# Cross-attention with folded weights: first weight loads by rows, context's rest turned by VectorE, Wv turned into a tile of its own

## The chip, the core and the metric

The kernel runs on one core of a Trainium2 chip. The core has five engines that run at the same time, each through its own list of instructions in order: TensorE (PE; its weight loads are shown apart as PEld), VectorE (DVE), ScalarE (ACT), GpSimd (POOL) and SyncE (SP), which here only issues DMAs. The metric is the device time of one execution in microseconds (us). The kernel before takes 280.88 us, the median of three runs (280.25 to 281.27).

## What is computed

Sixteen batches; x is 256 x 256 per batch, the context c is 77 x 192 per batch, with 8 heads of width 256. All in float32.

```python
Q = (x @ Wq)    # 256 -> 8 heads of 256
K = (c @ Wk)    # 192 -> 8 heads of 256
V = (c @ Wv)
score = einsum("bhqd,bhkd->bhqk", Q, K) / sqrt(256)
score = where(mask, score, -inf)
attn = softmax(score)
out = (attn @ V) @ Wo + x
y = (out - mean(out)) * rsqrt(var(out) + 1e-5) * gamma + beta
```

## The kernel before

Weights are folded first. For each head, `Wk` of the head times `Wq` of the head, transposed, gives a 192 x 256 matrix, kept as `gA` (its first 128 rows) and `gB` (its last 64); `Wv` times `Wo` of the head gives `uA` and `uB` in the same way. `Q`, `K` and `V` are never formed. The context is held transposed: `cA` has its first 128 features on the partitions, `cB` the last 64, twice (a copy on the other half of the partitions). `cRA` and `cRB` hold the columns of the last 13 keys of each batch.

The program has two parts. The first, some 57 us of the span, is the preparation, and the second is a loop over the 16 batches (scores, softmax, product with the values, sum with x, layer norm) with TensorE busy throughout. The loop's first instruction on TensorE is `scores` (tile ps, L313). The change lies in the preparation alone.

The schedule is by hand: each engine does its instructions in the order in which the program names them, and waits on semaphores for what it needs. On TensorE the preparation runs in this order:

1. Idle transposes of the identity (`keep_busy`, L605), 14 at first, until weights land.
2. `turn_k`, `turn_q`, `turn_k_last` (L619): the first two heads of each half of the eight are loaded in natural layout and transposed 128 x 128 by TensorE (tiles pt_k, pt_q, pt_kl); an ACT or DVE copy takes each result to `kT` or `qT`. The index e is a pair of neighbouring heads (heads 0 and 1, or 4 and 5), u the head in the pair, t the upper or lower 128 rows of Wq.
3. `g_of(e)` (tile pg, L723) and `rest_of_g(u)` (tile ph, L737): the folded products of these heads.
4. `turn_c` (tile pc, L657): the context's rows in `c_sb`, 112 to a row of tiles, are transposed by TensorE; ACT copies to `cA`, DVE to the upper half of `cB`, POOL from there to its lower half. The first call does 3 of the 11 rows, which is enough for the first four batches.
5. `a_of_places` (tile pa, L199 and L213): products of `gA` and `gB` with the context of the first four batches.
6. `of_pair` and `rest_of_pairs` (L680, L694) for the other heads of Wk and Wq (tiles pgb and phb). These weights come in blocks of 32 x 32, turned by DVE (`turn_blk`, L646) out of `wk_blk` and `wq_blk` into `kT_blk` and `qT_blk`.
7. Once more `a_of_places`, then `turn_c` for the other 8 rows.
8. The same `of_pair` and `rest_of_pairs` with Wv and Wo (tiles pu and pw). `turn_v` (L672) turns Wv's blocks in place in `wvT`; `wv_part` reads columns with a step of four elements.
9. `prepare_last` (tile pr, L274 and L284): `uA` and `uB` with `cRA` and `cRB`, into `vr`.

POOL meanwhile copies `cRA` and `cRB` (L784, L785), clears `vr` (L786), turns the mask into the additive `bias` (L790), copies halves of `uB` (L809), forms differences in `uA` and `uB` (L812, L813), and adds the mask's NaN rule to `bias` (L818), which the loop's first `shift` on DVE (L328) reads.

All loads are issued by SP on one queue, in program order: Wk and Wq for e = 0, then for e = 1, the last 64 rows of Wk (`wk_last`), three rows of context, the blocks of Wk and Wq, the other eight rows of context, Wv's blocks, Wo, mask, and the first group of x in blocks (`load_xT`). Eight semaphores are used in turn for them, so an issue waits until the eighth load before it has landed. PSUM has eight banks (`ps_mm`), reused in turn.

Of the kernel before, what the change touches and what calls it, by code (L numbers as in the profile page):

```python
# [8 lines left out]
F32 = mybir.dt.float32  # L9
I32 = mybir.dt.int32  # L10
AF = mybir.ActivationFunctionType
ALU = mybir.AluOpType
# [3 lines left out]
P = 128  # L16
H = 8
D = 256
EPS = 1e-05
GB = 4  # L20
KM = 64
MASKED = 3.0e38
# [31 lines left out]
def kernel(  # L54
# [13 lines left out]
    nc = tc.nc  # L68
    B, S, DI = x.shape
    S2, DL = c.shape[1], c.shape[2]  # L70
    LB = DL - P
    CR = 112
    NCR = B * S2 // CR
    NG = B // GB
    QT = S // P
    NT = B * QT
# [5 lines left out]
    NL = DL // BK  # L82
    PW = (NF + 1) * BK
    assert KM == 2 * BK and NM == NF and 2 * KR <= BK
    assert NCR * CR == B * S2 and NG * GB == B and DI == 2 * P and D == 2 * P and 2 * LB == P


    engines = mybir.EngineType
# [30 lines left out]
    cB = const.tile([P, B, S2], F32, tag="cB", name="cB")  # L119
    cRA = const.tile([P, B, KR], F32, tag="cRA", name="cRA")  # L120
    cRB = const.tile([P, B, KR], F32, tag="cRB", name="cRB")
    vr = const.tile([P, B, DI], F32, tag="vr", name="vr")
    p_ring = [const.tile([P, NM, PW], F32, tag=f"p{i}", name=f"p_{i}") for i in range(2)]
    for p in p_ring:
        nc.gpsimd.memset(p[:, :, 2 * S2 :], 0.0)
# [10 lines left out]
    def flat(ap):  # L136
        return ap.rearrange("p a b -> p (a b)")

    def half(i):
        return slice(i * LB, (i + 1) * LB)  # L140
# [7 lines left out]
    def evacuate(dst, src):  # L148
        evacs[0] += 1
        if evacs[0] % 2:  # L150
            nc.scalar.copy(dst, src)
        else:
            nc.vector.tensor_copy(dst, src)  # L153
# [18 lines left out]
    def transpose_x(g, j):  # L172

        cols = xT_of[g][:, j * NM : (j + 2) * NM]
        nc.vector.transpose(cols, cols)
# [368 lines left out]
    early = ctx.enter_context(tc.tile_pool(name="early", bufs=1))  # L544
    pools[0] = turned = early
    with tc.tile_pool(name="wonce", bufs=1) as wp:
        c_sb = wp.tile([CR, NCR, DL], F32, tag="c", name="c_sb")


        wq_nat = wp.tile([P, 2, 2, 2 * D], F32, tag="w128", name="wq_nat")  # L550
# [5 lines left out]
        wk_blk = wp.tile([P, 2, NL, P], F32, tag="wkb", name="wk_blk")  # L556
        wq_blocks = wq.rearrange("(m r) (a i f) -> a i r m f", r=BK, a=NF, i=NM)
        wk_blocks = wk.rearrange("(m r) (a i f) -> a i r m f", r=BK, a=NF, i=NM)
        wq_rows = wq.rearrange("(t p) (e f) -> e p t f", p=P, e=2)
        wk_rows = wk[:P].rearrange("p (e f) -> e p f", e=2)  # L560
        wk_ends = wk[P:].rearrange("r (e f) -> (r e) f", e=2)

        def load_blocks(to, blocks):
            for i in range(NM):
                nc.sync.dma_start(to[i * BK : (i + 1) * BK], blocks[i])

        def load_c(lo, hi):
            nc.sync.dma_start(c_sb[:, lo:hi, :], c_rows[:, lo:hi, :])

        first = -(-GB * S2 // CR)  # L570
        nc.sync.dma_start(wk_nat[:, 0], wk_rows[0][:, : 2 * D])
        nc.sync.dma_start(wq_nat[:, 0], wq_rows[0][:, :, : 2 * D])
        nc.sync.dma_start(wk_nat[:, 1], wk_rows[1][:, : 2 * D])
        nc.sync.dma_start(wq_nat[:, 1], wq_rows[1][:, :, : 2 * D])
        nc.sync.dma_start(wk_last, wk_ends[:, : 2 * D])
        load_c(0, first)
        for e in range(2):
            load_blocks(wk_blk[:, e], wk_blocks[2 * e + 1])
            load_blocks(wq_blk[:, e], wq_blocks[2 * e + 1])
        load_c(first, NCR)  # L580

        warm = const.tile([P, 1], F32, tag="warm", name="warm")
        nc.scalar.activation(warm, eps, AF.Exp)
# [8 lines left out]
            load_blocks(wvT[:, a], wv_blocks[a])  # L592
        for a in range(NF):
            nc.sync.dma_start(wo_of[a // 2][:, a % 2], wo_rows[a])
        nc.sync.dma_start(
            bias_f.bitcast(I32), mask.rearrange("b k -> (b k)").partition_broadcast(P)
        )
# [5 lines left out]
        def keep_busy(n):  # L603
            for i in range(n):
                nc.tensor.transpose(idle, ident, ident)  # L605

        keep_busy(14)


        qT = const.tile([P, 2, 2, 2, DI], F32, tag="xg0", name="qT")  # L610
# [4 lines left out]
        def turn_chunks(of, name):  # L615

            pt = ps_mm.tile([P, 4, P], F32, tag="mm", name=f"pt_{name}")
            for i, chunk in enumerate(of):
                nc.tensor.transpose(pt[:, i], chunk, ident)  # L619
            return pt  # L620

        def turn_q(e, u):
            chunks = [
                wq_nat[:, e, t, u * D + dc * P : u * D + (dc + 1) * P]
                for dc in range(2) for t in range(2)
            ]
            pt = turn_chunks(chunks, f"q_{e}_{u}")
            evacuate(flat(qT[:, e, u]), flat(pt))

        def turn_k(e):  # L630
            pt = turn_chunks([wk_nat[:, e, n * P : (n + 1) * P] for n in range(4)], f"k_{e}")
            evacuate(
                kT[:, e].rearrange("p u n l -> p (u n) l")[:, :, :P], pt
            )

        def turn_k_last():
            pt = turn_chunks([wk_last[:, n * P : (n + 1) * P] for n in range(4)], "kl")
            for e in range(2):
                evacuate(
                    kT[:, e].rearrange("p u n l -> p (u n) l")[:, :, P:],  # L640
                    pt.rearrange("p n (r e) -> p e n r", e=2)[:, e],
                )
# [5 lines left out]
                    blk[:, e].rearrange("p m (n c) -> p m n c", c=BK),  # L648
                )

        def turn_c(lo, hi):
            for r in range(lo, hi, 2):
                n = min(2, hi - r)
                pc = ps_mm.tile([P, 4, P], F32, tag="mm", name=f"pc_{r}")
                for lc in range(2):
                    for j in range(n):
                        nc.tensor.transpose(  # L657
                            pc[:, 2 * lc + j, :CR],
                            c_sb[:, r + j, lc * LB : lc * LB + P],
                            ident[:CR, :CR],  # L660
                        )
                rows = slice(r * CR, (r + n) * CR)
                evacuate(flat(cA)[:, rows].rearrange("p (j m) -> p j m", m=CR), pc[:, :n, :CR])
                evacuate(
                    flat(cB)[LB:, rows].rearrange("p (j m) -> p j m", m=CR),
                    pc[LB:, 2 : 2 + n, :CR],
                )
                nc.gpsimd.tensor_copy(flat(cB)[:LB, rows], flat(cB)[LB:, rows])  # L668

        def turn_v(a):  # L670
            blocks = wvT[:, a].rearrange("p m (c n) -> p m n c", n=4)
            nc.vector.transpose(blocks, blocks)  # L672

# [34 lines left out]
            return kT_blk[half(e), a, n]  # L710

        def wv_part(a, e, n):
            return flat(wvT[half(e), a]).rearrange("p (l n) -> p n l", n=4)[:, n]

        def wo_part(a, e, n):
            return wo_of[a // 2][half(e), a % 2, n, :]
# [1 line left out]
        def g_of(e):  # L718

            pg = ps_mm.tile([P, 2, DI], F32, tag="mm", name=f"pg_{e}")  # L720
            for u in range(2):
                for dc in range(2):
                    nc.tensor.matmul(  # L723
                        pg[:, u],
                        kT[:, e, u, dc, :P],
                        qT[:, e, u, dc],
                        start=(dc == 0),
                        stop=(dc == 1),
                    )
            nc.scalar.mul(gA[:, NF * e : NF * e + 2], pg, D ** -0.5)  # L730
# [20 lines left out]
                evacuate(dst, src)  # L751

        turn_k(0)
        keep_busy(4)
        turn_q(0, 0)
        turn_q(0, 1)
        turn_k(1)
        g_of(0)
        turn_q(1, 0)
        turn_q(1, 1)  # L760
        turn_k_last()
        turn_c(0, first)
        g_of(1)
        rest_of_g(0)
        rest_of_g(1)
        turn_blk(0)
# [13 lines left out]
        nc.sync.dma_start(bet, beta.partition_broadcast(P))  # L780
        a_of_places((2, 3))
        turn_v(3)
        turn_c(first, NCR)
        nc.gpsimd.tensor_copy(cRA, cA[:, :, KM:])  # L784
        nc.gpsimd.tensor_copy(cRB, cB[:, :, KM:])  # L785
        nc.gpsimd.memset(vr, 0.0)  # L786

        nc.gpsimd.tensor_scalar(bias_f, bias_f.bitcast(I32), 0.0, -MASKED, ALU.is_equal, ALU.mult)  # L790

        for j in range(NF // 2):
            pu = two_banks("pu", j)
            for a in range(2 * j, 2 * j + 2):
                of_pair(pu, a, wv_part, wo_part)
            for e in range(2):
                evacuate(
                    of_e(uA, e)[:, :, 2 * j : 2 * j + 2].rearrange("p n a c -> p a n c"),
                    pu[e].rearrange("p a (n c) -> p a n c", c=BK),
                )  # L800
        for j in range(NF // 2):
            for e, pw in enumerate(
                rest_of_pairs(j, (2 * j, 2 * j + 1), wv_part, wo_part, "pw")
            ):
                for i, engine in enumerate((nc.scalar.copy, nc.vector.tensor_copy)):
                    a = 2 * j + i
                    here, there = (of_e(uB, e)[half(k), :, a] for k in (i, 1 - i))
                    engine(here, pw[half(i)].rearrange("p (n c) -> p n c", c=BK))
                    nc.gpsimd.tensor_copy(there, here)  # L809
        for u in (uA, uB):  # L810
            t2, _, b22, b11, b12 = (u[:, q].rearrange("p n i c -> p (n i c)") for q in range(5))
            nc.gpsimd.tensor_tensor(t2, b22, b12, ALU.subtract)  # L812
            nc.gpsimd.tensor_tensor(t2, t2, b11, ALU.add)  # L813
        nan = wp.tile([P, B, 1], F32, tag="nan", name="nan")
        nc.vector.tensor_reduce(nan[:, :, 0], bias, AX.X, ALU.max)
        nc.gpsimd.tensor_tensor(nan, nan, nan, ALU.mult)
        nc.gpsimd.tensor_tensor(nan, nan, nan, ALU.subtract)
        nc.gpsimd.tensor_tensor(bias, bias, nan.to_broadcast([P, B, S2]), ALU.add)  # L818

        for j in range(0, GT, 2):  # L820
            transpose_x(0, j)
        prepare_last()


# [131 lines left out]
```

## Time and profile before

| what | before |
|---|---|
| median of 3 runs | 280.88 us (280.25 to 281.27) |
| the profiled execution, its own time | 279.81 us |
| its span, first to last instruction | 278.0 us |
| TensorE busy | 269.4 us (97%) |
| VectorE busy | 206.6 us (74%) |
| ScalarE busy | 166.6 us (60%) |
| GpSimd busy | 167.8 us (60%) |
| first instruction of the main loop on TensorE (ps) | 56.62 us |
| granted TensorE clock, mean | 0.993 |

The times in all views count from the first instruction of the profiled execution. The chain of waits is followed back from the last instruction: each piece is either work on an engine, or a DMA, or an issue, that the next piece waited for. A group of instructions is a line of the program on one engine with its tiles and shapes: total busy time, mean time of one, and the idle time ahead of them with what ended most of it. TensorE's matmuls overlap, so the mean of one is longer than its share of the time; for them the time of a whole piece of the chain is used. The number of matmul records is twice the program's for float32 products and once for transposes.

### The profile page before, as it was taken

The numbers are of one execution on the slowest core, as the hardware profiler recorded it, in microseconds if no ns is written. First come the engines' busy times: TensorE is split into PE (matmuls) and PEld (weight loads), VectorE is DVE, ScalarE is ACT, GpSimd is POOL, SyncE is SP. The second block draws the span as 40 slices with busy tenths as digits, with TensorE's granted clock in tenths as the row PEclk, the third lists the DMA queues.
The fourth block names the chain that finished last, engine by engine and source line by source line (L and its number), as shares of the span: only waits on it lengthen the run. The fifth ranks groups of instructions, "written<-read, shape, count | busy, mean of one in ns | idle before, by whom it ended". The sixth has DMA issues, their size and how long they took to land.

```text
span 278.0 us, 13274 instructions
## 1 busy us (share of the span) xinstructions
PE 269.4 (97%) x5924; PEld 194.2 (70%) x5924; DVE 206.6 (74%) x423; ACT 166.6 (60%) x447; POOL 167.8 (60%) x226
## 2 busy tenths in 40 slices
PE   7999999999999999999999999999999999999991
PEld 6756499976595959585868686868677767575650
DVE  0463952777838898878889787778788887788785
ACT  2303232146638676767767676868585857869761
POOL 1000069946677777787877878777777536335274
PEclk9999999999999999999999999999999999999997
DMA  6997999930000100950100109500001010010103
GB/s 192 249 230 154 308 261 238 204 105 4 2 6 2 35 10 24 189 174 4 42 2 5 41 5 193 180 16 22 24 2 42 2 40 14 31 41 2 40 4 113
DMA packets 35641, 22.61 MB, mean 81 GB/s; under 512 B 17712, under 2 KB 34048, under 8 KB 35584
## 3 DMA queue, kind: packets, MB, share of 16 engines
q1 hardware_dynamic: 35440, 21.64, 30.8%
q8 instruction: 46, 0.75, 1.2%
q10 hardware_dynamic: 144, 0.13, 0.1%
q14 instruction: 11, 0.09, 0.1%
HBM read 17.57 MB, written 4.19 MB: 78 GB/s over the span
## 4 chain that ended last, share of the span: by engine, by line
PE 89%; DVE 4%; DMA 3%; ACT 2%; SPq 1%; POOL 0%; issue 0%; POOLq 0%; ACTq 0%
PE ps L313 23%; PE pa L199 12%; PE pv L241 9%; PE po L429 9%; PE pm L429 7%; PE pa L213 6%; PE pv L252 6%; PE po L378 5%; DMA c_sb<-in_ctx_dram 3%; PE pu L680 3%; PE pr L274 2%; ACT e L342 2%; PE pw L694 1%; PE pgb L680 1%; PE pr L284 1%; PE pc L657 1%
## 5 line engine op out<-in xcount | busy, mean ns | idle before, releaser
L342 ACT ACTIVATE e<-s,top 128x77 f32<-128x77 f32 x256 | 67.1, 347 | 52.1 <-DVE top L335 49.9
L356 POOL TENSOR_TENSOR p<-e,rden 128x512 f32<-128x512 f32 x64 | 45.9, 739 | 46.5 <-DVE rden L350 46.3
L313 PE MATMUL ps<-a,xT 128*32 128x154 f32 x2048 | 70.0, 294 | 0.0
L313 PEld LDWEIGHTS ps<-a,xT 128*32 128x32 f32 x2048 | 66.1, 110 | 1.7 <-issue 0.7
L328 DVE TENSOR_TENSOR s<-ps,bias 128x308 f32<-128x308 f32 x64 | 30.3, 475 | 17.6 <-PE ps L313 15.9
L199 PE MATMUL pa<-cA,gA 128*32 128x308 f32 x512 | 35.8, 423 | 0.0
L462 POOL TENSOR_TENSOR xg<-xg,m 128x256 f32<-128x256 f32 x33 | 24.2, 734 | 13.5 <-DVE xg L476 11.8
L199 PEld LDWEIGHTS pa<-cA,gA 128*32 128x32 f32 x512 | 16.4, 110 | 20.9 <-issue 8.0
L241 PE MATMUL pv<-uA,cA 128*32 128x512 f32 x256 | 30.4, 592 | 0.0
L366 DVE STREAM_TRANSPOSE pT<-p 128x640 f32<-128x640 f32 x32 | 25.6, 824 | 2.4 <-POOL p L356 2.4
L348 DVE TENSOR_REDUCE den<-e 128x8 f32<-128x616 f32 x32 | 24.7, 772 | 3.5 <-ACT e L342 3.5
L335 DVE TENSOR_REDUCE top<-s 128x8 f32<-128x616 f32 x32 | 25.4, 795 | 1.1
L668 POOL COPY cB<-cB 64x224 f32<-64x224 f32 (+1 forms) x6 | 1.9, 360 | 35.2 <-DVE cB L153 35.2
L392 POOL TENSOR_TENSOR ts<-vw 128x768 f32<-128x768 f32 x11 | 22.0, 1997 | 0.0
L213 PE MATMUL pa<-cB,gB 64*32 64x308 f32 x512 | 19.5, 420 | 0.0
L378 PE MATMUL po<-vw,pT 128*32 128x256 f32 x320 | 19.2, 380 | 0.0
L863 ACT COPY vw<-pv 128x512 f32<-128x512 f32 x32 | 16.9, 579 | 2.5 <-PE pv L252 2.5
L495 ACT ACT_TABLE_LOAD x14 | 18.0, 1283 | 0.3
L213 PEld LDWEIGHTS pa<-cB,gB 64*32 64x32 f32 x512 | 9.7, 107 | 11.3 <-issue 7.6
L252 PE MATMUL pv<-uB,cB 64*32 64x512 f32 x256 | 17.4, 601 | 0.0
L516 DVE SCALAR_TENSOR_TENSOR xg<-xg,mv,gam 128x256 f32<-128x256 f32 x25 | 17.2, 688 | 0.0
L378 PEld LDWEIGHTS po<-vw,pT 128*32 128x32 f32 x320 | 10.0, 110 | 9.5 <-DVE den L348 2.5
(115 smaller groups left out, 444.0 us busy)
## 6 DMA issues: line engine op xcount, KB each, us to landing
xT<-in_x_dram SPq DMA_DIRECT2D x16, 256.0 KB, 6.1
xg<-in_x_dram SPq DMA_DIRECT2D x4, 1024.0 KB, 7.6
out_dram<-xg SPq DMA_DIRECT2D x15, 256.0 KB, 2.3
wo<-in_L_xattn_Wo_dram SPq DMA_DIRECT2D x4, 512.0 KB, 5.9
wvT<-in_L_xattn_Wv_dram SPq DMA_DIRECT2D x16, 96.0 KB, 3.0
wq_nat<-in_L_xattn_Wq_dram SPq DMA_DIRECT2D x2, 512.0 KB, 6.0
wq_blk<-in_L_xattn_Wq_dram SPq DMA_DIRECT2D x8, 128.0 KB, 4.7
wk_blk<-in_L_xattn_Wk_dram SPq DMA_DIRECT2D x8, 96.0 KB, 5.5
```

Of the source, the lines that this page charges most:

```text
L199: nc.tensor.matmul(flat(o[i * BK : (i + 1) * BK]), gA[:, h, cols(dc, i)], flat(cA[:, batches, :]), start=not B_first, stop=B_first,)
L213: nc.tensor.matmul(flat(banks[j + k][i * BK : (i + 1) * BK]), gB[half(k), h % NF, cols(dc, i)], flat(cB[half(k), batches, :]), start=B_fir ...
L241: nc.tensor.matmul(pv[k][i * BK : (i + 1) * BK], cA[:, b, k * BK : (k + 1) * BK], uA[:, parts, :, i], start=True, stop=False,)
L252: nc.tensor.matmul(pv[k][i * BK : (i + 1) * BK], cB[half(k), b, k * BK : (k + 1) * BK], uB[half(k), parts, :, i], start=False, stop=True,)
L313: nc.tensor.matmul(ps[m // 2][i * BK : (i + 1) * BK, m % 2 * 2 * S2 : (m % 2 + 1) * 2 * S2], xT_of[g][:, j * NM + m, dc], flat(a_of[g][:, ...
L328: nc.vector.tensor_tensor(s[:, a * H // 2 : (a + 1) * H // 2], ps[a][:, : H // 2 * S2].rearrange("p (h k) -> p h k", k=S2), bias[:, b, :]. ...
L335: nc.vector.tensor_reduce(top, s, AX.X, ALU.max, negate=True)
L342: nc.scalar.activation(e[:, h], s[:, h], AF.Exp, bias=top[:, h : h + 1])
L356: nc.gpsimd.tensor_tensor(part, e_mh[:, :, :, keys], rden_mh.unsqueeze(3).to_broadcast(list(part.shape)), ALU.mult,)
L366: nc.vector.transpose(pT_of[t].rearrange("p n m q -> p m n q"), p.rearrange("p m (n k) -> p m n k", k=BK),)
L378: nc.tensor.matmul(po[i * BK : (i + 1) * BK], pT[:, n, i], vw_of[b][:, 2 - n // 2 * 2 : 4 - n // 2 * 2, n % 2, :] if n < NF else vr[:, b, ...
L429: nc.tensor.matmul(out[i * BK : (i + 1) * BK], weight[:, i], moving, start=(n == 0), stop=(n == len(terms) - 1),)
```

## The change

It has three parts, and edits that follow from them.

- The first loads of Wk and Wq now take both pairs of heads (e = 0 and 1) in one piece for each row: one load for Wk and one for each half t of the rows of Wq, three in place of four. `turn_q` follows: it takes one t and one e, and the order on TensorE is turn_k(0), turn_k(1), two idle transposes, four turn_q, turn_k_last, g_of(0), g_of(1), turn_c, rest_of_g. The first idle transposes are 16.
- The context's rest (eight rows of 112) is no longer loaded into `c_sb` and turned by TensorE. Six loads after Wo's bring blocks of 32 x 32 straight to `cA` and the upper half of `cB`; two DVE transposes turn them in place, POOL makes the lower half of `cB` with one copy, and `cRA` and `cRB`. DVE does this after the first evacuation of pu.
- `turn_v` writes a tile of its own, `wv_turned`, in the place of `vr`, so that `wv_part` reads contiguous columns; `vr` is allocated later and its unused columns are cleared by DVE after the transposes of x.
- The mask's conversion to `bias` moves from POOL to DVE, between the evacuations of pu and pw. The NaN rule on POOL moves ahead of the differences in `uA` and `uB`.

```diff
-        wq_rows = wq.rearrange("(t p) (e f) -> e p t f", p=P, e=2)
-        wk_rows = wk[:P].rearrange("p (e f) -> e p f", e=2)
+        wq_rows = wq.rearrange("(t p) (e f) -> t p e f", p=P, e=2)[:, :, :, : 2 * D]
+        wk_rows = wk[:P].rearrange("p (e f) -> p e f", e=2)[:, :, : 2 * D]
...
-        nc.sync.dma_start(wk_nat[:, 0], wk_rows[0][:, : 2 * D])
-        nc.sync.dma_start(wq_nat[:, 0], wq_rows[0][:, :, : 2 * D])
-        nc.sync.dma_start(wk_nat[:, 1], wk_rows[1][:, : 2 * D])
-        nc.sync.dma_start(wq_nat[:, 1], wq_rows[1][:, :, : 2 * D])
+        rest = slice(first * CR, None)
+        def load_rest():
+            blocks = c.rearrange("b k l -> (b k) l")[rest].rearrange("(m r) l -> r m l", r=BK)
+            for l in range(NL):
+                i, of = (l, cA) if l < NM else (l - NM + LB // BK, cB)
+                nc.sync.dma_start(
+                    flat(of)[i * BK : (i + 1) * BK, rest].rearrange("p (m q) -> p m q", q=BK),
+                    blocks[:, :, l * BK : (l + 1) * BK],
+                )
+        def turn_rest():
+            nc.vector.transpose(flat(cA)[:, rest], flat(cA)[:, rest])
+            nc.gpsimd.tensor_copy(cRA, cA[:, :, KM:])
+            nc.vector.transpose(flat(cB)[LB:, rest], flat(cB)[LB:, rest])
+            nc.gpsimd.tensor_copy(flat(cB)[:LB, rest], flat(cB)[LB:, rest])
+            nc.gpsimd.tensor_copy(cRB, cB[:, :, KM:])
+        nc.sync.dma_start(wk_nat, wk_rows)
+        for t in range(2):
+            nc.sync.dma_start(wq_nat[:, t], wq_rows[t])
         nc.sync.dma_start(wk_last, wk_ends[:, : 2 * D])
-        load_c(0, first)
+        nc.sync.dma_start(c_sb, c_rows[:, :first, :])
...
-        load_c(first, NCR)
...
             nc.sync.dma_start(wo_of[a // 2][:, a % 2], wo_rows[a])
+        load_rest()
...
-        keep_busy(14)
+        keep_busy(16)
...
-        def turn_q(e, u):
-            chunks = [
-                wq_nat[:, e, t, u * D + dc * P : u * D + (dc + 1) * P]
-                for dc in range(2) for t in range(2)
-            ]
-            pt = turn_chunks(chunks, f"q_{e}_{u}")
-            evacuate(flat(qT[:, e, u]), flat(pt))
+        def turn_q(t, e):
+            chunks = [wq_nat[:, t, e, n * P : (n + 1) * P] for n in range(4)]
+            pt = turn_chunks(chunks, f"q_{t}_{e}")
+            evacuate(
+                qT[:, e].rearrange("p u n d -> p (u n) d")[:, :, t * P : (t + 1) * P], pt
+            )
...
+        wv_turned = const.tile([P, NF, 4, DL], F32, tag="vr", name="wv_turned")
         def turn_v(a):
-            blocks = wvT[:, a].rearrange("p m (c n) -> p m n c", n=4)
-            nc.vector.transpose(blocks, blocks)
+            nc.vector.transpose(
+                wv_turned[:, a].rearrange("p n (m r) -> p m n r", r=BK),
+                wvT[:, a].rearrange("p m (c n) -> p m n c", n=4),
+            )
...
-            return flat(wvT[half(e), a]).rearrange("p (l n) -> p n l", n=4)[:, n]
+            return wv_turned[half(e), a, n]
...
         turn_k(0)
-        keep_busy(4)
-        turn_q(0, 0)
-        turn_q(0, 1)
         turn_k(1)
+        keep_busy(2)
+        for t in range(2):
+            for e in range(2):
+                turn_q(t, e)
+        turn_k_last()
         g_of(0)
-        turn_q(1, 0)
-        turn_q(1, 1)
-        turn_k_last()
-        turn_c(0, first)
         g_of(1)
+        turn_c()
...
-        turn_c(first, NCR)
-        nc.gpsimd.tensor_copy(cRA, cA[:, :, KM:])
-        nc.gpsimd.tensor_copy(cRB, cB[:, :, KM:])
-        nc.gpsimd.memset(vr, 0.0)
-        nc.gpsimd.tensor_scalar(bias_f, bias_f.bitcast(I32), 0.0, -MASKED, ALU.is_equal, ALU.mult)
...
+            if j:
+                turn_rest()
...
+        nc.vector.tensor_scalar(bias_f, bias_f.bitcast(I32), 0.0, -MASKED, ALU.is_equal, ALU.mult)
...
+        vr = const.tile([P, B, DI], F32, tag="vr", name="vr")
+        ends = flat(vr).rearrange("p (n c) -> p n c", c=BK)[:, :, 2 * KR :]
+        nc.vector.memset(ends, 0.0)
         prepare_last()
```

More of the change, by code (lines that the diff above doesn't have):

```diff
@@ L72 @@
     CR = 112
-    NCR = B * S2 // CR
     NG = B // GB
@@ L84 @@
     assert KM == 2 * BK and NM == NF and 2 * KR <= BK
-    assert NCR * CR == B * S2 and NG * GB == B and DI == 2 * P and D == 2 * P and 2 * LB == P
+    assert NG * GB == B and DI == 2 * P and D == 2 * P and 2 * LB == P
     engines = mybir.EngineType
@@ L121 @@
     cRB = const.tile([P, B, KR], F32, tag="cRB", name="cRB")
-    vr = const.tile([P, B, DI], F32, tag="vr", name="vr")
     p_ring = [const.tile([P, NM, PW], F32, tag=f"p{i}", name=f"p_{i}") for i in range(2)]
@@ L546 @@
     with tc.tile_pool(name="wonce", bufs=1) as wp:
-        c_sb = wp.tile([CR, NCR, DL], F32, tag="c", name="c_sb")
+        first = -(-GB * S2 // CR)
+        c_sb = wp.tile([CR, first, DL], F32, tag="c", name="c_sb")
         wq_nat = wp.tile([P, 2, 2, 2 * D], F32, tag="w128", name="wq_nat")
@@ L565, in load_blocks @@
                 nc.sync.dma_start(to[i * BK : (i + 1) * BK], blocks[i])
-        def load_c(lo, hi):
-            nc.sync.dma_start(c_sb[:, lo:hi, :], c_rows[:, lo:hi, :])
-        first = -(-GB * S2 // CR)
-        nc.sync.dma_start(wk_nat[:, 0], wk_rows[0][:, : 2 * D])
-        nc.sync.dma_start(wq_nat[:, 0], wq_rows[0][:, :, : 2 * D])
-        nc.sync.dma_start(wk_nat[:, 1], wk_rows[1][:, : 2 * D])
-        nc.sync.dma_start(wq_nat[:, 1], wq_rows[1][:, :, : 2 * D])
+        rest = slice(first * CR, None)
+        assert (B * S2 - first * CR) % BK == 0
+        def load_rest():
[15 more added lines that the diff above has]
+            nc.sync.dma_start(wq_nat[:, t], wq_rows[t])
         nc.sync.dma_start(wk_last, wk_ends[:, : 2 * D])
-        load_c(0, first)
+        nc.sync.dma_start(c_sb, c_rows[:, :first, :])
         for e in range(2):
@@ L649, in turn_blk, with turn_c @@
                 )
-        def turn_c(lo, hi):
-            for r in range(lo, hi, 2):
-                n = min(2, hi - r)
+        def turn_c():
+            for r in range(0, first, 2):
+                n = min(2, first - r)
                 pc = ps_mm.tile([P, 4, P], F32, tag="mm", name=f"pc_{r}")
@@ L809 @@
                     nc.gpsimd.tensor_copy(there, here)
[L810 to L813, printed above, removed]
         nan = wp.tile([P, B, 1], F32, tag="nan", name="nan")
@@ L818 @@
         nc.gpsimd.tensor_tensor(bias, bias, nan.to_broadcast([P, B, S2]), ALU.add)
+        for u in (uA, uB):
+            t2, _, b22, b11, b12 = (u[:, q].rearrange("p n i c -> p (n i c)") for q in range(5))
+            nc.gpsimd.tensor_tensor(t2, b22, b12, ALU.subtract)
+            nc.gpsimd.tensor_tensor(t2, t2, b11, ALU.add)
         for j in range(0, GT, 2):
             transpose_x(0, j)
+        vr = const.tile([P, B, DI], F32, tag="vr", name="vr")
+        ends = flat(vr).rearrange("p (n c) -> p n c", c=BK)[:, :, 2 * KR :]
+        nc.vector.memset(ends, 0.0)
         prepare_last()
```

## The prediction

> **What bounds the kernel now.** I read the page's summary first, then the chain of waits, then the groups of instructions in the first 66 us by shape, then the DMA queue by time.
>
> ```profile
> span 278.0 us, 13274 instructions
> PE 269.4 (97%) x5924; PEld 194.2 (70%) x5924; DVE 206.6 (74%) x423; ACT 166.6 (60%) x447; POOL 167.8 (60%) x226
> ```
>
> TensorE is busy 97% of the span and the chain puts 89% on it. So a change pays only in what it does to TensorE's own list of work and to the holes in it. The chain of waits in order of time (start, length, what) shows both:
>
> ```profile
> 2.61 0.47 SPq L575
> ...
> 3.12 8.36 DMA c_sb<-in_ctx_dram
> ...
> 11.53 0.80 PE pc L657 x6
> 12.32 1.74 PE pg L723 x8
> 14.06 1.88 PE ph L737 x16
> 15.94 4.29 PE pa L199 x64
> 20.23 2.23 PE pa L213 x64
> 22.46 3.65 PE pgb L680 x32
> 26.12 1.89 PE phb L694 x32
> 28.00 4.28 PE pa L199 x64
> 32.29 2.23 PE pa L213 x64
> 34.52 1.68 PE pc L657 x16
> 36.20 7.77 PE pu L680 x64
> 43.98 3.68 PE pw L694 x64
> 47.65 3.01 PE pr L274 x16
> 50.66 3.01 PE pr L284 x32
> 53.68 3.01 PE pr L274 x16
> 56.69 4.33 PE ps L313 x128
> ```
>
> Until 11.5 us a landing decides, the first three rows of context. From there TensorE never stops until the tail at 256 us; ps at 56.69 is the first of the main loop, which the diff leaves alone. So what counts is how far the start of ps moves: the main loop and tail follow it one for one, if nothing new is late.
>
> **Context's rest off TensorE: -1.68 us.** turn_c's second call (pc at 34.52, x16) leaves TensorE's list. Its ACT and DVE evacuations and POOL's four copies go with it; two DVE transposes, one bulk POOL copy and six DMAs come in their place, priced below.
>
> **Wv into its own tile: -0.5 us.** At first sight this looks larger:
>
> ```profile
> L680 PE MATMUL pu<-wo,wvT 64*128 64x256 f32 x64 | 7.8, 400 | 0.0
> L680 PEld LDWEIGHTS pu<-wo,wvT 64*128 64x128 f32 x64 | 7.5, 325 | 0.1
> L680 PE MATMUL pgb<-qT_blk,kT_blk 64*128 64x256 f32 x32 | 3.7, 382 | 0.0
> L680 PEld LDWEIGHTS pgb<-qT_blk,kT_blk 64*128 64x128 f32 x32 | 3.0, 187 | 0.8 <-ACT a L151 0.5
> ```
>
> pgb is the same code with contiguous weights, which wv_turned will give pu: the weight load falls from 325 to 187 ns. But loads overlap matmuls, and pgb has half as many: 3.65/32 = 0.114 us per matmul against 7.77/64 = 0.121. The saving is 7.77 - 2 x 3.65 = 0.47 us, taken as 0.5. pw is no slower now than its contiguous twin phb (3.68 against 2 x 1.89), so 0. The DVE transposes should fall too, from 1.64 us (wvT in place, strided) to the 0.95 of kT_blk (128x768, contiguous out). That saves nothing on the path: before, they ended at 36.7 with nothing of TensorE waiting.
>
> **The first loads: +0.7 us, the part against the change.** Now a load holds one pair of heads, so g_of(0) (1.74 us) ran at 7.75 to 9.48 in a hole, before the second half of Wq landed (issued 2.14, 7.1 us to landing: 9.24). After, neither g_of can start before the last Wq tile: every head pair needs both. From that landing L, TensorE has 8 transposes (0.93), turn_k_last (0.47; wk_last lands at about L + 1.0, in time; the ACT copy that g_of(0) waits for ends at L + 1.35, hidden by it), two g_of (3.47), pc (0.63) and ph to the start of pa (1.97, from start to start). Sum 7.5 us, so pa starts at L + 7.5. Today it starts at 15.87. Context has landed by then (11.5) and is no longer what holds.
>
> L is the unknown. The bytes ahead are the same: 512 KB of Wk and 1024 of Wq, packets still 2 KB. One issue of 0.45 us fewer stands ahead. Upper end: L = 9.5, if the longer single loads spread worse over the engines. Lower end: L = 7.8, if the 307 GB/s that the window view shows at 2 to 3 us held throughout (1.57 MB / 0.307 = 5.1 us from 1.9 us on, and 0.8 of lag as in the first landing); actually it drops to 225 and 215 GB/s at 4 to 6 us. Since packet size and bytes do not change, I take the row as it is, less a part of the issue: L = 9.1, pa at 16.6, +0.7 us. The ends give +1.1 and -0.6. The idle transposes (16 and 2 for 14 and 4) end near 4.75, when Wk's double load lands (first load 3.5 us, plus 256 KB at about 215 GB/s): 0.
>
> The hole ahead of L is about 1 us instead of 0.5. The Trainium skill (TensorE: Matmul & The Clock Gate, Part 1) has the array fall back to half clock after an idle window of about 3.4 us; this trace's holes of 0.5 us cost no speed. By the rule and by the row the cost is 0; had the clock fallen, the 12 transposes and 16 matmuls behind L would cost about 4 us more. A 1 us hole is nearer the row.
>
> **The queue of DMAs.** Each issue on SP waits for the landing of the eighth before it. Before, the rest of context (672 KB, issued 15.85, landed 23.6) stood ahead of Wv, and SP sat up to 3.0 us on it; DMA throughput fell to 82 and 55 GB/s at 24 to 26 us. After, Wv follows Wq's blocks directly (last landing 20.3): 1.5 MB at about 210 GB/s end at 27.8 instead of 31.0, and the four Wo loads, 1.4 us each, at 33.3 instead of 37.7. pu needs Wo's first at 35.1, so cover is ample. Then the six load_rest pieces: 32 rows x 28 x 32 floats, 896 packets of 128 B each, 336 packets per engine in all.
>
> The trace has no 128 B packet. Row: the xT loads have 256 B packets, 64 per engine and load; by issue plus time to landing they land 1.46 us apart at 41.6 to 45.9 and 1.63 at 51.7 to 56.6: 23 to 25.5 ns each. At the same price a packet the rest takes 7.7 to 8.6 us. Rule: the skill (DMA: Bandwidth & Descriptors, Why small descriptors are slow) counts bytes/32 + 3 cycles a packet, 7 against 11, which makes it 14.6 to 16.2 ns and 5.2 us; the same page (Specifications) warns of read-modify-write under 512 B. Estimate 6 us (18 ns), nearer the row's overhead-bound end; ends 4.9 and 8.6. So the rest lands at R = 39.3 (38.2 to 41.9). Mask follows at R + 2.6 (2.9 now, after Wo) = 41.9 (to 44.5), and xT, four at 1.5, by about 48.
>
> **Who waits for it.** With pa at 16.6, TensorE's list gives pu 35.1 to 42.4, pw to 46.1, pr's three parts to 55.2. DVE in order: uA of the first pu (ready 38.8), transpose of cA (128x896: 1.07 us between 0.95 for 768 and 1.22 for 1024), of cB (1.07), uA of the second (42.5), mask to bias (128x1232: 1.45, as the reduce of the same width at 1.44; on POOL it was 4.39), four uB copies, the reduce, four xT transposes (2.5), the memset (about 0.9), ended near 52. The cA transpose waits for four of the six pieces, due at 37.3; behind it stand the uA and uB copies that pr needs. Pieces are there when DVE comes at 39.5. POOL copies cRA, cB (64x896: 0.8, from 0.28 for 112 and 0.36 for 224), cRB, then eight uB copies as they come, done near 48.3. pr's part B starts at 46.1 + 3.0 = 49.1, so 0.8 us of slack (before, 0.3 of waiting, since POOL's 4.39 us bias row and 3.51 us memset ended at 47.2). The bias sum (0.44 + 2.25) moves ahead of the u differences and ends at 51.3; the first shift needs it at 57.3, where before DVE waited 1.6 us for it. The differences end at 56.4, pv reads them at 59.4. xT's transposes end by 51 and ps needs them at 55.2. The early release of Wv's tile lets xT of the second group be issued sooner; needed about 90 us. All 0.
>
> **Sum.** -1.68 - 0.5 + 0.7 = -1.5 us. Against the profiled execution: 279.81 - 1.5 = 278.3 (span 278.0 to 276.5). That execution was 1.1 us below the 280.88 median of the three runs; I forecast the median: 280.88 - 1.5 = **279.4**.
>
> **Rivals.** (a) *The first loads run faster.* Both pieces of a row together may keep memory busier: L = 7.8, gain 2.18 + 0.6 = 2.8, time 278.1. For it: the dip to 215 GB/s and a 2.3 us spread between first and last engine of a load leave room. Against: same packets, same bytes. 15%.
> (b) *The hole is lost for nothing.* L = 9.5 or later and half the pu gain: 1.68 + 0.25 - 1.1 = 0.8, and a 0.3 us wait at part B: 0.5, time 280.4, not to be told from no change. 18%.
> (c) *Slower: the 128 B packets delay mask, DVE stands on it.* Part B can start when the bias row (1.45), the first DVE uB copy and seven POOL copies are through, mask + 4.75. It stalls once mask lands after 49.1 - 4.75 = 44.35, that is R over 41.75 or 25.4 ns a packet, and eats the 1.5 us from 29.9 ns on. At double the row's price (46 ns), R = 48.8, mask 51.4, a stall of 7 us: 286.4. For it: read-modify-write, and contention the rest meets for the first time. Against: 256 B at 23 to 25.5 ns. 11%.
> (d) *That it doesn't do it:* TensorE's new list has the 16 transposes gone, so only pu's part could fail, which (b) holds.
>
> **Numbers.** Forecast 56%, a 15%, b 18%, c 11%. Faster by over 0.3% (0.84 us, about what this measurement tells from none): 0.56 + 0.15 = 0.71; same 0.18; slower 0.11. Range: low from (a), 278.0; high past (b), 280.8; left out are (c), and the edges of (a) and (b), some two in ten.
>
> **What would show it.** pc only x6 and before ph; pg x16 in one run from about L + 1.4; pa at 16.6; pu near 7.3 with loads of 187 ns; ps near 55.2. Wrong if pa starts past 17.5, if wq_nat's last landing is far from 9.1, or if an idle row "PEld pr <- POOL uB" or "PE pr <- DVE" of a microsecond appears, with DVE idle before the cA transpose or the bias row.

## The result, and the profile after

The changed kernel takes **279.13 us**, the median of 20 runs (277.28 to 283.79), against 280.77 (279.91 to 281.99) for the kernel before, 20 runs. The ratio is 0.9938 with a 95% interval of 0.9917 to 0.9959. The ratio leaves out executions more than 1.5% above a kernel's fastest, here four of the changed kernel; the medians and the counts of executions below leave out none.

The median is 0.3 us from the forecast of 279.4. The spread is not what the kernel before has: 6.5 us in place of 2.1. The profiled execution of the changed kernel is one of the long ones, 283.14 us with a span of 281.4 and a mean granted clock of 0.985. These are lines of its page: the summary and the granted clock in fortieths of the span.

```profile
span 281.4 us, 13235 instructions
...
PE 270.8 (96%) x5908; PEld 195.1 (69%) x5908; DVE 209.1 (74%) x423; ACT 165.2 (59%) x443; POOL 159.5 (57%) x221
...
PEclk9779999999999999999999999999999999999998
```

TensorE has 16 records fewer, the transposes of context's rest, and yet is busy 1.4 us longer. The two 7s in the clock row, from 7 to 21 us, say why. The chain of waits of the same execution (start, length, what) shows where:

```profile
2.09 9.38 DMA wq_nat<-in_L_xattn_Wq_dram
...
11.52 1.97 PE pt_q L634 x8
13.48 0.85 PE pt_kl L634 x4
14.34 4.84 PE pg L742 x16
19.18 0.58 PE pc L671 x6
19.75 1.88 PE ph L756 x16
21.63 4.29 PE pa L197 x64
...
40.21 7.11 PE pu L699 x64
47.32 3.61 PE pw L713 x64
...
59.97 4.32 PE ps L311 x128
```

pc stands once, x6, ahead of ph, and pu follows pa directly: the rest's transposes are gone, and pu is at 7.11 us for the 7.77 of before. But Wq's last landing is at 11.47, 2.4 us past the 9.1 forecast, and the pieces behind it run too long: pg's 16 products take 4.84 us where two g_of took 3.47. The windows view of the same execution (stretch, its length, busy time and count of PE, PEld, DVE, ACT, POOL, then the granted clock, DMA share, GB/s) puts the clock beside the holes:

```profile
10.00:12.00 2.00, 0.67 (x5) 0.49 (x4) 0.69 (x1) 0.37 (x1) 0.00 (x0) 0.55 1.09 137
12.00:14.00 2.00, 2.00 (x11) 2.00 (x11) 0.48 (x1) 0.59 (x1) 0.00 (x0) 0.50 0.63 176
```

By the trace's clock record the array falls to half clock at 10.19 us and is at full clock again from 17.02. So pa starts 10.1 us after Wq's landing in place of 7.5.

The sum on TensorE's list behind that stretch can be read from pa to ps, which the clock no longer touches: 56.62 - 15.87 = 40.75 us before, 59.90 - 21.56 = 38.34 after (starts of the first instructions in the timeline). That is **-2.41 us**, against -1.68 - 0.5 = -2.18 forecast.

### The profile page after: what moved, and what is told of

It reads as the page before. It is cut to its first block, busy times and chain, and to the rows that moved or that the text cites. A ratio compares the mean times of both kernels' runs of the same rounds, so it can differ in the third digit from the quotient of the medians.

```text
span 281.4 us, 13235 instructions
## 1 busy us (share of the span) xinstructions
PE 270.8 (96%) x5908; PEld 195.1 (69%) x5908; DVE 209.1 (74%) x423; ACT 165.2 (59%) x443; POOL 159.5 (57%) x221
## 4 chain that ended last, share of the span: by engine, by line
PE 89%; DVE 4%; DMA 3%; ACT 1%; POOL 0%; SPq 0%; issue 0%; POOLq 0%; ACTq 0%
PE ps L311 23%; PE pa L197 12%; PE pv L239 9%; PE po L427 9%; PE pm L427 7%; PE pa L211 6%; PE pv L250 5%; PE po L376 5%; DMA wq_nat<-in_L_xattn_Wq_dram 3%; PE pu L699 3%; PE pr L272 2%; PE pg L742 2%; ACT e L340 1%; PE pgb L699 1%; PE pw L713 1%; PE pr L282 1%
## 5 line engine op out<-in xcount | busy, mean ns | idle before, releaser
L326 DVE TENSOR_TENSOR s<-ps,bias 128x308 f32<-128x308 f32 x64 | 30.4, 475 | 17.6 <-PE ps L311 17.5
L197 PEld LDWEIGHTS pa<-cA,gA 128*32 128x32 f32 x512 | 17.5, 110 | 19.8 <-issue 7.4
L333 DVE TENSOR_REDUCE top<-s 128x8 f32<-128x616 f32 x32 | 25.5, 795 | 1.1
L881 ACT COPY a<-pa 128x308 f32<-128x308 f32 x48 | 16.6, 446 | 0.0
```

What stands on the lines that cost most here:

```text
L197: nc.tensor.matmul(flat(o[i * BK : (i + 1) * BK]), gA[:, h, cols(dc, i)], flat(cA[:, batches, :]), start=not B_first, stop=B_first,)
L326: nc.vector.tensor_tensor(s[:, a * H // 2 : (a + 1) * H // 2], ps[a][:, : H // 2 * S2].rearrange("p (h k) -> p h k", k=S2), bias[:, b, :]. ...
```

## The experiments

The theory after the result: TensorE's list is 2.4 us shorter, and the new head loses part of it, in some executions much of it, to the clock. The rivals: the head costs nothing and the rest's DMAs or DVE's new work take time back; or the long executions have nothing to do with the change. The runs are of three batches, each with the kernel before beside it: again, head_back, rest_back and wv_back (before: 280.59 us, 60 runs), then, on another chip, before_again, g_late, fill and c_last (280.25, 50) and the last three (280.16, 40). The changed kernel itself was timed again in the first batch only, so what follows compares ratios across batches.

| run | median us (range), runs | ratio to before, 95% | clock fell in |
|---|---|---|---|
| before_again | 280.54 (279.33 to 283.76), 22 | 1.0007 (0.9995 to 1.0020) | 0 of 22 |
| again | 279.90 (277.48 to 283.61), 22 | 0.9956 (0.9934 to 0.9978) | 8 of 22 |
| head_back | 279.08 (278.42 to 279.82), 7 | 0.9949 (0.9932 to 0.9967) | 0 of 7 |
| rest_back | 281.57 (279.13 to 285.41), 22 | 1.0022 (1.0002 to 1.0042) | 8 of 22 |
| wv_back | 281.59 (278.07 to 283.91), 22 | 0.9987 (0.9966 to 1.0008) | 12 of 22 |
| g_late | 279.64 (278.02 to 283.00), 16 | 0.9976 (0.9950 to 1.0002) | 5 of 16 |
| fill | 279.42 (277.46 to 281.62), 19 | 0.9960 (0.9941 to 0.9978) | 0 of 19 |
| c_last | 277.78 (277.01 to 278.42), 6 | 0.9908 (0.9889 to 0.9927) | 0 of 6 |
| rest_alone | 278.90 (278.29 to 279.90), 10 | 0.9953 (0.9936 to 0.9971) | 0 of 10 |
| wv_alone | 279.75 (279.12 to 281.08), 22 | 0.9981 (0.9968 to 0.9993) | 0 of 22 |
| split_loads | 279.18 (278.52 to 280.39), 15 | 0.9972 (0.9958 to 0.9987) | 0 of 15 |

"Clock fell" counts executions whose mean granted clock is below 0.993, which is the lowest that any of the 172 of the kernel before in these batches shows (a stretch of half clock at the very end, when TensorE has little or nothing left to do, is in the mean). Of the 20 runs of the changed kernel in the result it fell in 5.

**The changed kernel and the kernel before, once more.** No edit.

> The changed kernel once more, for a profile of another execution. In the one at hand the last Wq tile landed at 11.47 us and the array fell back to half clock from 10.2 to 17.0 us. Theory 1 (the sum of the prediction holds in a typical execution): Wq lands near 9.1, no half clock after the first idle transposes, pa starts near 16.6 and ps near 55.2; time 279.3. Theory 2 (the new head is unsettled, late landing and half clock come in many executions): Wq past 10 us again, times spread over more than 3 us, pa past 17.5.

> The kernel before once more, for a second profile of it. Both theories of the head: the same time, 280.6; the three rows of context land near 11.5 to 12 us, ps starts near 56.6 to 57.1, no half clock after the first idle transposes. Open: whether its loop also has a hole near 120 us at the load of the third group of x, which the first profile of it did not show (0.03 us) and every profile with the new preparation does (0.3 to 1.7 us). If the hole comes in this one, it belongs to both kernels; if not, it is a loss of the change.

In this profile of the changed kernel, again, the clock held. Its chain of waits:

```profile
2.09 6.59 DMA wq_nat<-in_L_xattn_Wq_dram
...
10.43 3.46 PE pg L742 x16
...
16.34 4.28 PE pa L197 x64
...
34.91 7.11 PE pu L699 x64
...
54.67 4.32 PE ps L311 x128
```

The same load lands at 8.68 here and at 11.47 above, and pa starts 7.6 us behind it, as the sum had it (7.5). This is the change as forecast; the other profile is the change with a late landing and a fallen clock. Over both sets the clock fell in 13 of 42 executions, all at 281.1 us or above; the other 29 have medians of 278.87 and 279.30, some 1.9 and 1.3 us under the kernel before of their batch. It fell in none of the 172 of the kernel before: the falls belong to the change. (Two executions of before_again are long as well, 282.29 and 283.76 us, at a clock that held; their cause is open.)

**The head of before in the changed kernel (head_back).**

```diff
-        nc.sync.dma_start(wk_nat, wk_rows)
-        for t in range(2):
-            nc.sync.dma_start(wq_nat[:, t], wq_rows[t])
+        nc.sync.dma_start(wk_nat[:, 0], wk_rows[0][:, : 2 * D])
+        nc.sync.dma_start(wq_nat[:, 0], wq_rows[0][:, :, : 2 * D])
+        nc.sync.dma_start(wk_nat[:, 1], wk_rows[1][:, : 2 * D])
+        nc.sync.dma_start(wq_nat[:, 1], wq_rows[1][:, :, : 2 * D])
...
         turn_k(0)
+        keep_busy(4)
+        turn_q(0, 0)
+        turn_q(0, 1)
         turn_k(1)
...
         g_of(0)
+        turn_q(1, 0)
+        turn_q(1, 1)
+        turn_k_last()
+        turn_c()
         g_of(1)
```

> The changed kernel with the head of before: four loads by pairs of heads, 14 and 4 idle transposes, g_of(0) between the halves. Theory 1: the new head costs 0.7 us, so this is 0.7 us faster than the changed kernel, 278.6, with pa at 15.9 and ps at 54.5. Theory 2: the same or more is gained, 1 to 2 us, and the times spread as little as before's, about 1.5 us. Theory 3 (the double loads are faster and pay): 0.5 to 1 us slower than the changed kernel.

Wq's last landing is at 9.63, the clock never fell, and the whole range is 1.4 us. Yet pa starts at 16.38, no earlier than the 16.27 of the changed kernel at full clock: the context, which holds this head, lands 0.5 us later than before (12.00). So the new head is no slower when its loads come early; what it costs is the executions in which they don't. They give nearly all of the 0.8 us by which again's median is longer (its executions with the clock up have 279.30, only 0.2 more), and the spread.

**The rest by TensorE again (rest_back), Wv in place again (wv_back), each in the changed kernel.**

```diff
-        load_rest()
...
+        turn_c(first, NCR)
...
-            if j:
-                turn_rest()
```

> The changed kernel with context's rest loaded behind Wq's blocks and turned by TensorE again. Theory 1: TensorE gets its 16 transposes back, pu starts 1.7 us later, time 1.7 us above the changed kernel, 281.0. Rival: the small packets' landing or the DVE turns already cost part of it, so the difference is under 1 us.

```diff
-            nc.vector.transpose(
-                wv_turned[:, a].rearrange("p n (m r) -> p m n r", r=BK),
-                wvT[:, a].rearrange("p m (c n) -> p m n c", n=4),
-            )
+            blocks = wvT[:, a].rearrange("p m (c n) -> p m n c", n=4)
+            nc.vector.transpose(blocks, blocks)
...
-            return wv_turned[half(e), a, n]
+            return flat(wvT[half(e), a]).rearrange("p (l n) -> p n l", n=4)[:, n]
```

> The changed kernel with Wv turned in place again and read with a step of four elements. Theory 1: pu takes 7.8 us instead of 7.1 to 7.3, time 0.5 us up, 279.8, hardly told from the changed kernel. Rival: weight loads of 325 ns hold back more than pu's matmuls, 1 us or more.

The pieces return. A line of the chain of rest_back:

```profile
39.20 1.68 PE pc L655 x16
```

and two of the chain of wv_back:

```profile
39.44 7.78 PE pu L695 x64
47.21 3.68 PE pw L709 x64
```

So the rest is worth 1.68 and Wv 0.67 + 0.07 = 0.74 us of TensorE's list. The medians do not say so: in both profiles the clock had fallen, and so it did in 8 and 12 executions. The others, which it does not touch, have medians of 281.02 and 279.65 against 279.30 of again, 1.7 and 0.35 us; for Wv that is less than the list has, with 10 and 14 executions compared. To measure the parts without that noise they were tried on the head of before.

**Each part alone, on the kernel before.** rest_alone is head_back with Wv in place (the edit of wv_back). wv_alone is the kernel before with `wv_turned`, and the mask, NaN rule and `vr` as after the change.

> The kernel before with the context part alone (six blocks loads, DVE's turns, mask on DVE, vr late); head and Wv as before. On the settled head its size should stand free of the half clock: by the sum 1.68 us, time 280.4 less 1.7 = 278.7, ps at 55 where context's first rows land at 11.5 to 12. Rival: under 1 us, if the small packets or DVE's turns hold something back.

> The kernel before with Wv's own tile alone (and the mask on DVE and vr late, which have no place on TensorE's path); head and context's rest as before. By the sum 0.5 us, by pu's time in the later profiles (7.11 against 7.78) and pw's (3.61 against 3.68) 0.7: time 279.7 to 279.9.

No clock fell in either. Measured are -1.3 us for the rest (interval 0.8 to 1.8; the loop of its profile is 0.9 us longer, see the last section) and -0.5 (0.2 to 0.9) for Wv. From pa to ps the rest takes 55.31 - 16.25 = 39.06 (-1.69) and Wv 56.64 - 16.62 = 40.02 (-0.73): -2.42 together, what the changed kernel shows. On TensorE's list the parts add up, and neither is taken back ahead of ps.

**The hole filled (fill).** Only idle transposes are added, so that TensorE has work while Wq lands.

```diff
-        keep_busy(2)
+        keep_busy(8)
         for t in range(2):
             for e in range(2):
                 turn_q(t, e)
+            if t == 0:
+                keep_busy(8)
```

> The changed kernel with more idle transposes in its holes: 8 in place of 2 behind turn_k, and 8 between the two halves of turn_q. Theory A: the clock stays up, the times above 282.5 go, median 279.0 to 279.5, the fastest runs lose up to 0.5 us. Theory B: the late landing stays, so the slow runs shrink only by the half clock's part, some 3 of their 5 us; runs at 280 to 281 remain.

The timeline of TensorE in its profile (start, length, engine, line, operation, tiles, forms, count, and in brackets the idle time before it and what ended it):

```profile
8.20 1.09 PE L634 MATMUL pt_q<-ident,wq_nat 128*128 128x128 f32 x8 [1.06 <-DMA wq_nat<-in_L_xattn_Wq_dram]
9.12 1.04 PE L620 MATMUL idle<-ident 128*128 128x128 f32 x8
10.34 1.09 PE L634 MATMUL pt_q<-ident,wq_nat 128*128 128x128 f32 x8 [0.18 <-DMA wq_nat<-in_L_xattn_Wq_dram]
...
12.29 3.62 PE L742 MATMUL pg<-qT,kT 128*128 128x256 f32 x16
```

The load is late here too, 10.30, and the transposes and products run at full speed all the same: 1.09 and 3.62 us. No execution of 19 fell, against 13 of 42 of the changed kernel; the longest is 281.62. (The changed kernel was not timed in this batch; g_late, which was, on the same chip, fell in 5 of 16.) So the fall comes from the holes. The ratio is the changed kernel's, 0.996: a late landing still costs its own time, as in this profile, where pa starts at 18.29.

**The landing (split_loads).** The order of rows is kept, but each double load is issued as two of 256 KB.

```diff
-        nc.sync.dma_start(wk_nat, wk_rows)
+        for e in range(2):
+            nc.sync.dma_start(wk_nat[:, e], wk_rows[:, e])
         for t in range(2):
-            nc.sync.dma_start(wq_nat[:, t], wq_rows[t])
+            for e in range(2):
+                nc.sync.dma_start(wq_nat[:, t, e], wq_rows[t][:, e])
```

> The changed kernel with its order on TensorE kept, and each of its three double loads issued as two of 256 KB, one pair of heads each. If the shape of the double loads makes the last Wq tile land late (10.3 to 11.7 us in four of five profiles, 9.2 to 9.9 in the five with loads of before), it lands near 9.6 to 10 here and the low clock is rarer, times like g_late's, median 279.1 to 279.6. If the order by row halves t does it, or chance, it lands past 10.3 again and the low clock stays in about 3 of 10 executions.

Its last landing is at 9.54, and the clock never fell in 15. Last landings of Wq in all profiles: 9.24 to 9.94 us in the seven with the loads of before; 8.68, 10.30, 10.73, 11.47 and 11.71 in the five with double loads. That points to the shape of a load, over the same bytes and packets of 2 KB, but it is one profile against five, and one of the five is early. The trace shows what is late: each load leaves 16 landing marks. Of the last Wq load in the changed kernel's first profile, eight have come by 7.29 us (8.24 in the kernel before), and the last is 4.6 us behind the first, for 2.3 in the kernel before and 1.5 in again. So a few parts of the load are late, not all of it; why isn't shown. The comparison is not clean either: split_loads has three loads more in the row of eight semaphores. Its pa starts at 17.25, 7.7 us behind L, held by wk_last's landing at 10.71.

**Where g_of(0) and g_of(1) stand (g_late, c_last).** g_late is head_back with two lines moved, c_last with one.

```diff
 # g_late
-        g_of(0)
         turn_q(1, 0)
         turn_q(1, 1)
         turn_k_last()
+        g_of(0)
+        g_of(1)
         turn_c()
-        g_of(1)
 # c_last
         turn_k_last()
+        g_of(1)
         turn_c()
-        g_of(1)
```

> The changed kernel with the four loads of before by pairs of heads, but g_of(0) only behind turn_k_last, as in the change. It parts the shape of the loads from the place of g_of(0). Theory A (the hole and its clock do it): TensorE has as little to do before the last Wq tile as in the changed kernel, half clock in some executions, times spread over 4 us and more, median 1 us above head_back's 279.1. Theory B (the double loads land late by themselves): Wq lands at 9.2 to 9.7, no half clock, times within 2 us, median 279.8 to 280.2, the 0.7 to 1.1 us of the sum and no more.

> The changed kernel with the head of before and one swap: g_of(1) ahead of turn_c, so that TensorE works while the three rows of context are still on the way. By the sum TensorE then runs without a hole from the last Wq tile on: L + 0.97 for the transposes of q, turn_k_last, g_of(1), turn_c, ph, pa at L + 6.0 = 15.3 to 15.7 instead of 16.4 in head_back: 0.8 us below it, 278.3, with as little spread. Rival: context lands last anyway and holds turn_c, gain under 0.3.

g_late has the loads of before but the order of the change, with nothing in the hole ahead of the second half of Wq: the clock fell in 5 of 16, up to 283.00 us. So it is the hole, by whichever means, that lets the clock fall. c_last keeps g_of(0) in that hole, as head_back does, and puts g_of(1) ahead of the context, which then no longer holds the chain:

```profile
2.63 8.46 DMA wk_last<-in_L_xattn_Wk_dram
...
11.23 0.63 PE pt_kl L635 x4
11.86 1.73 PE pg L744 x8
...
16.04 4.29 PE pa L197 x64
...
54.38 4.32 PE ps L311 x128
```

The last rows of Wk hold it now, and TensorE runs from 11.23 without a hole. **277.78 us** in 6 runs, ratio 0.9908 (0.9889 to 0.9927), beats the kernel before and is the lowest ratio here; the changed kernel has 0.9938 and 0.9956, in other batches and with intervals that overlap its own or lie close to it. By the ratios it is 1.1 us below head_back (each with an interval of about 0.5 us to either side), while its profile shows 0.4 us at ps (54.31 for 54.72); what the rest is, one profile of each does not tell.

## Why the prediction was right, point by point

- **Context's rest, -1.68**: right; the piece is gone (1.68 in the chain of rest_back) and nothing took it back ahead of ps.
- **Wv's tile, -0.5 and 0 for pw**: right in kind, somewhat small. pu came to 7.11 instead of 7.30, and pw fell by 0.07; 0.74 in all. The twin with half as many instructions was a fair row, though twice its 3.65 us is 0.2 more than the 7.11 measured; where those 0.2 lie was not looked into. The weight loads came out as said, 187 ns for pu in the tile view of again (operation, tiles, count: minimum/median/maximum in ns, first and last start, form):

```profile
L699 PEld LDWEIGHTS pu<-wo,wv_turned x64: 182/187/187, 34.8 to 41.4; 64*128 64x128 f32 x64
```

- **turn_v on DVE, 1.64 to 0.95**: wrong. It stays at 1.55 to 1.63. Only the destination became contiguous; the source is still read with a step, which kT_blk's is not. It cost nothing, as it is hidden.
- **The first loads, +0.7**: the step that failed. Right was the sum behind L (7.6 measured for 7.5 at full clock in again), with one term short: wk_last was in time there (9.73), but in g_late, fill and split_loads it landed 1.2 to 1.5 us behind Wq and held the chain, 7.7 to 8.0 us from L to pa. Wrong was the upper end of 9.5 for L, taken from the row of the separate loads; four of five profiles with double loads lie past it, by the uneven spread that the prediction itself named. And wrong was the step "By the rule and by the row the cost is 0; had the clock fallen, the 12 transposes and 16 matmuls behind L would cost about 4 us more." The clock did fall in 13 of 42 executions. Its price was less than that: in the profiled one L to pa took 10.1 us for 7.5, so 2.6 for the clock, which came back within pg, and 2.4 more for the late landing; there pa starts at 21.6, past the 17.5 that the forecast named as a sign against it. The effect on the median is small, some 0.8 us against head_back in the same batch, so the forecast of the median held. That it held to 0.3 us is in part luck: TensorE's list gained 0.2 more than forecast, the clock, put at nothing, took time in three executions of ten, and again, the same kernel, has 279.90.
- The rule there, an idle window of about 3.4 us (the Trainium skill, TensorE: Matmul & The Clock Gate, Part 1), was read too kindly. The changes of the clock stand in its record at 6.78 (the first entry, full clock), 10.19 and 17.02 us, steps of one and two times 3.41 us, which agrees with such a window. But a window that is only mostly idle was enough, and no single hole was over 2.05 us. These are windows of this execution, of rest_back (two) and of wv_back (behind the length stands TensorE's busy time):

```profile
6.78:10.19 3.41, 1.35 (x10) 0.86 (x8) 0.69 (x1) 0.40 (x1) 0.00 (x0) 1.00 1.09 264
...
4.48:7.89 3.41, 1.66 (x13) 1.18 (x11) 0.69 (x1) 0.59 (x1) 0.00 (x0) 1.00 0.80 264
7.89:11.31 3.42, 1.10 (x8) 0.86 (x8) 0.69 (x1) 0.59 (x1) 0.00 (x0) 1.00 1.17 228
...
5.97:9.38 3.41, 1.50 (x13) 1.26 (x12) 0.69 (x1) 0.68 (x2) 0.00 (x0) 1.00 1.00 284
```

  Half clock follows the windows with 1.35, 1.10 and 1.50 us of work, and not the one with 1.66. Cut in this way from each clock record's first entry, all thirteen profiles agree: at full clock, all 16 windows with at most 1.50 us of work, 13 of them at the end of a kernel, were followed by half clock, and none with 1.56 us or more. Where the windows lie differs from one execution to the next (the first entry stands anywhere from 4.14 to 7.17 us). But in the profiles of the kernels that never fell, no stretch of this length in the preparation from 3.5 us on, wherever it is laid, has under 1.87 us of work (2.18 in fill), and in again, with its early landing, none has under 1.96. So in the changed kernel it takes a late landing to make the hole wide enough.
- **The rest's DMAs, 18 ns a packet, R = 39.3, mask 41.9**: right. In again the last piece lands at 39.06 and Wo's last at 33.43: 5.63 us / 336 packets = 16.8 ns, near what the rule gives (14.6 to 16.2) and well below the row (23 to 25.5). The mask landed at 41.45. (Rival (c)'s limit of R = 41.75 works out, by the prediction's own terms, at 25.1 ns a packet and not 25.4, and its 29.9 at 29.6; what was measured is clear of all four.)
- **DVE and POOL hide their new work**: right. The timeline of DVE in again:

```profile
39.25 1.10 DVE L581 STREAM_TRANSPOSE cA<-cA 128x896 f32<-128x896 f32 x1
40.38 1.11 DVE L583 STREAM_TRANSPOSE cB<-cB 64x896 f32<-64x896 f32 x1
42.10 0.69 DVE L151 COPY uA<-pu 128x512 f32<-128x512 f32 x1 [0.60 <-PE pu L699]
42.82 0.80 DVE L815 TENSOR_SCALAR bias<-bias 128x1232 f32<-128x1232 int32 x1
```

  Both transposes took 1.1 us (1.07 forecast). The bias row starts behind the mask's landing without an idle time, and takes 0.80 us, not 1.45. DVE waits for pu here, not pu for DVE. The one idle row of the forecast's test, pr's weight loads for POOL's uB copy, has 0.4 us, and TensorE itself had no hole there. So rival (c), with DVE stuck on the mask, fell.
- **The loop follows one for one**: not quite. From its first ps to the last it took 199.4 us in the kernel before and 200.96 in again, see the last section; that, not the preparation, is what keeps the gain between these two profiles (span 278.0 to 277.2) below the 2.0 us that ps moved (56.62 to 54.60).
- Rival (a), faster loads: the one early landing, 8.68, lies between its 7.8 and the forecast's 9.1. Rival (b), the hole lost, was nearest to what the head does: L past 9.5. Its other halves (half the gain of pu, a wait at part B) did not come.

## What to carry to other kernels

A hole on TensorE in the ramp-up can cost more than its length. Here the clock fell where a window of 3.41 us held no more than 1.5 us of work, though no single hole was longer than 2.05 us in the profile shown, and since both the windows and the landings move, the loss is paid in some executions only: look at the spread and the granted clock of every run before trusting one profile. Put useful work that is ready early, here g_of(0), into such a hole and, where there is none, idle instructions. Merging loads saves issues but lets more work wait for the last of the larger pieces, and its landing has to be measured, not taken from the smaller ones.

## What the runs showed of the hardware beyond that

The loop, which no edit touches, is 0.2 to 1.7 us longer in most of these profiles than the 199.43 of the kernel before (before_again 199.98, rest_alone 200.32, head_back 200.29, rest_back 201.12; wv_alone and split_loads 199.42 and 199.43). In again the excess lies in two iterations around 120 us, in which TensorE's timeline has idle times with no releaser, 0.9 us of the 1.5:

```profile
121.30 0.53 PE L427 MATMUL po<-ts,pT 128*32 128x128 f32 x11 [0.59 <-issue]
...
125.85 1.11 PE L311 MATMUL ps<-a,xT 128*32 128x154 f32 x27 [0.29 <-issue]
```

Just then the third group of x is loaded, and on the queue that brings instructions no packet of 16 KB starts between 110.9 and 118.9 us; in the kernel before the same gap is 111.7 to 117.7. Over the profiles the loss follows this gap: nothing to 0.2 us where it is under 7 us, 0.3 to 1.7 where it is 7.3 to 9.6, the most at 9.6 (rest_back). That TensorE waits for instructions held up behind data is what this suggests; it was not tried. Since before_again has it as well (gap 8.2 us, loss 0.55), it is not the change's own.
